# Two copies of a scratch image, zero rows around it, and products on all 128 rows

## The chip, the cores and the metric

The kernel runs on one core of a Trainium2 chip. The time is the device time of one launch in microseconds (us). The profile is one further execution, recorded by the hardware profiler. Engines are written as in the profile: PE (matrix products), DVE (vector), ACT (scalar), POOL (GpSimd), SP (which here only starts DMAs).

## The reference

Input `x` is 4 x 16 x 256 x 256 in float32. Two layers follow each other, each with a residual:

```python
x = x + _L0_conv_ref(_gn(x), conv_w, conv_b)          # _gn: group norm over 8 groups of 2 channels
x = x + _L1_conv_ref(_gn(x), base_w, spl_w, scaler, bias)

# layer 0: a 3x3 convolution 16 -> 400 gives 25 logits per channel and pixel
weights = softmax(out.reshape(N, C, 25, H, W), axis=2)
y = einsum('ncuij,ncuij->ncij', unfold5x5(x), weights)

# layer 1: a 3x3 convolution of silu, and of 8 cubic B-splines, of the normalised image
out = einsum('bjhwn,ijn->bihw', silu(patches), base_weight.sum(2))
out += einsum('bjhwns,ijns->bihw', b_splines(patches), (spline_weight * scaler).sum(2))
out += bias
```

## The kernel before

**Setup** (to about 108 us) loads the input, takes the statistics of the first norm, normalises the first image and prepares the weights: `wt` for the splines and `ws` for silu and the residual, both with 128 partitions.

**Layer 0** works in 64 strips: 4 images, 2 halves of 128 rows (one row per partition), 8 strips of 32 columns. Every four columns are one step, 512 in all. PE makes the logits, two products per column (L878 on `am`, L882 on `an`) into `lg`; ACT takes the exponential (L901) into `e`; POOL multiplies it by the shifted images `u` (L906); DVE sums numerator and denominator into `nd` (L738). Some steps later the strip is divided (ACT L752 and L754, DVE L758 to L760) and POOL subtracts it from the input's tile `xc` (L766), which then holds the first layer's result, x1. The products' operands come in chunks of eight columns, 256 of them, loaded two chunks ahead: `load_im` issues five DMAs (three of `am` at L686, two of `an` at L696) on SP's queue. Once per strip `load_u` issues five DMAs (L710), and `load_xc` one per four strips (L716), on the same queue. In between, pieces of the next image's normalisation are issued (`normalize`, lines up to L405, with loads at L288 to L319 on SP).

After every fourth strip `xc` is complete, with 128 rows x 16 channels x 128 columns. `store` (L820) writes it to the scratch `x1s`, 1 MB in rows of 512 B. Fifteen of these stores are issued on ACT's queue and the last on POOL's. ACT takes the statistics of the second norm from the same tile (L786). The DMAs that SP and ACT issue share eight semaphores in turn, in program order, so that a DMA waits until the one eight places before it has landed.

**Layer 1** works in 64 units of 16 rows of an image. All 128 partitions hold 16 channels x 8 spline knots of the unit's 18 rows. `load_x` (L988) loads them from `x1s` in two halves, the eight knots' copies by a dimension of step 0, into the first free of three tiles (`xta`, `xtb`, `xtc`); `load_tiles` (L1003) loads the rows once more into partitions 64 to 127 of `sl`, in four blocks of 16 partitions, block k with the rows of one of four row offsets in the order 0, 1, 3, 2. Rows outside the image are set to zero by POOL memsets (L999, L1023). Loads run two units ahead:

```python
xtt[n % 3][:, a - lo : z - lo, :],
rows(x1s[b], [[CP, C], [0, NS], [1, (z - a) * W]], u * RU - 1 + a),
```

ACT takes the distance to the knots (Abs, L1036), silu from the upper half of `sl` into its lower half (L1018), and parts of the splines (L164 to L167); DVE makes the rest (L159, L168 to L170) into `ring`. PE multiplies: 48 products on `ring` (L1082) and 12 on `sl` (L1092), these on 128 rows only for the middle column tap, where `ws` also adds the residual, else on 64. DVE adds the bias (L1065) and SP stores 2 x 128 KB (L1072).

`layer1` begins as layer 0 ends. The tile `xtc` lies where layer 0's `xc` tiles were, so its first load waits until the last store has landed. `scales` turns the second norm's statistics into per-partition factors `q` for every image, with one product on `sel` that spreads 16 channels over 128 partitions.

Of the kernel before, what the change touches and what calls it, by code (L numbers as in the profile page):

```python
# [4 lines left out]

# [30 lines left out]
def conv_preact_kernel(  # L36
# [12 lines left out]
    nc = tc.nc  # L49
    B, C, H, W = x.shape  # L50
    G = 8
    GC = C // G
    P = 128
# [6 lines left out]
    NS = 8  # L60
# [5 lines left out]
    CX = 128  # L66
# [6 lines left out]
    QG = 4  # L73
    RT = 2
    NT = P // (RT * C)
    RD = RT + 2
    RU = 16
    NU = H // RU
    SROWS = (0, 1, 3, 2)
    LAG1 = 2  # L80

    const = ctx.enter_context(tc.tile_pool(name="const", bufs=1))
# [5 lines left out]
    hsl = [[dram.tile([C, 2, CT], F32, name=f"hsl{b}_{h}") for h in range(NH)] for b in range(B)]  # L88

    CP = H * W + 1024  # L90
    x1s = [dram.tile([C, CP], F32, name=f"x1s{b}") for b in range(B)]
    ones = const.tile([P, P], F32, name="ones")
    nc.vector.memset(ones, 1.0 / P)
    mhalf = const.tile([P, G], F32, name="mhalf")
    nc.vector.memset(mhalf, -0.5)
    ub = const.tile([P, 1], F32, name="ub")
    ubrow = const.tile([1, C, NS], F32, name="ubrow")
    for s in range(NS):
        nc.vector.memset(ubrow[:, :, s : s + 1], 3.5 - s)
    ident = const.tile([P, P], F32, name="ident")  # L100
    make_identity(nc, ident)

    sel = const.tile([C, C, NS], F32, name="sel")
    nc.vector.tensor_copy(sel, ident[0:C, 0:C].unsqueeze(2).to_broadcast([C, C, NS]))
    onec = const.tile([P, 1], F32, name="onec")
    nc.vector.memset(onec, 1.0)
    flag = const.tile([1, 1], mybir.dt.int32, name="flag")
# [15 lines left out]
    ws = const.tile([P, 3, RT, C], F32, name="ws")  # L123
    nc.gpsimd.memset(ws, 0.0)
    for r in range(RT):
        p = P // 2 + SROWS.index(r + 1) * C
        nc.sync.dma_start(ws[p : p + C, 1, r], ident[p : p + C, p : p + C])

    edge = const.tile([P, 5], F32, name="edge")
    stat1 = ctx.enter_context(tc.tile_pool(name="stat1", bufs=1))  # L130
# [43 lines left out]
    def scales(b, psum):  # L174


        def small(n, name):
            return stat1.tile([P, n], F32, name=f"{name}_{b}", tag=f"{name}{b % 2}")

        sums, d, mz, p = small(2 * G, "sums"), small(G, "d"), small(G, "mz"), small(G, "p")  # L180
        q = stat1.tile([P, 6], F32, name=f"q_{b}", tag=f"q{b}")
        nc.vector.tensor_reduce(sums, st1[b].rearrange("p t g k -> p (t g) k"), AX.X, ALU.add)
        yield
        ps = psum()[:, 0 : 2 * G]
        nc.tensor.matmul(ps, lhsT=ones, rhs=sums, start=True, stop=True)
        yield
        part = 1.0 / (GC * CX * NK)
        nc.scalar.activation(d, ps[:, 0:G], AF.Square, scale=part)
        yield

        nc.vector.scalar_tensor_tensor(mz, ps[:, 0:G], part, nrm[b][:, 1], ALU.mult, ALU.subtract)
        nc.vector.scalar_tensor_tensor(d, ps[:, G : 2 * G], part, d, ALU.mult, ALU.subtract)  # L192
        yield
        nc.gpsimd.tensor_add(d, d, nrz[b][:, 1])  # L194
        nc.gpsimd.tensor_tensor(p, d, mhalf, ALU.pow)
        nc.gpsimd.tensor_mul(d, p, nrz[b][:, 0])
        nc.gpsimd.tensor_mul(p, p, gsel_sb)
        nc.gpsimd.tensor_mul(p, p, mz)
        yield
        nc.vector.reduce_sum(q[:, 0:1], d, AX.X)  # L200
        nc.vector.reduce_sum(q[:, 1:2], p, AX.X)
        nc.vector.tensor_scalar(q[:, 1:2], q[:, 1:2], -1.0, None, ALU.mult)
        for k in range(2):
            nc.vector.tensor_scalar(q[:, 2 + k : 3 + k], q[:, k : k + 1], 2.5, None, ALU.mult)
        yield
        ps = psum()[:, 0:2]
        nc.tensor.matmul(
            ps, lhsT=sel.rearrange("p c s -> p (c s)"), rhs=q[0:C, 2:4], start=True, stop=True
        )
        yield  # L210
        nc.vector.tensor_copy(q[:, 4:5], ps[:, 0:1])
        nc.vector.tensor_add(q[:, 5:6], ps[:, 1:2], ub)
        sc[b] = tuple(q[:, k : k + 1] for k in (0, 1, 4, 5))
        yield

    sc = {}
# [31 lines left out]
    def zeros(b, queue):  # L248

        for e in (0, HP - PAD):  # L250
            for r in range(PAD):
                yield partial(
                    queue.dma_start,
                    hs[b][:, e + r].rearrange("s c w -> c s w"),
                    zero[0:C, 0 : NST * SP].rearrange("c (s w) -> c s w", s=NST),
                )
        for h in range(NH):
            for w in (0, (W + 1) * RP):
                yield partial(queue.dma_start, hst[b][h][:, w : w + RP], zero[0:C, 0:RP])
                yield partial(  # L260
                    queue.dma_start,
                    hsl[b][h][:, :, w : w + RP].rearrange("c t r -> (c t) r"), zero[:, 0:RP],
                )
# [178 lines left out]
    with tc.tile_pool(name="prep0", bufs=2) as prep, tc.tile_pool(  # L442
# [42 lines left out]
        for d in range(3):  # L485
# [10 lines left out]

        ups = pstat.tile([P, 1], F32, name="ups", tag="hps")
        nc.tensor.matmul(
            ups, lhsT=ubrow.rearrange("p c s -> p (c s)"), rhs=onec[0:1], start=True, stop=True
        )  # L500
        nc.vector.tensor_copy(ub, ups)
        nc.scalar.activation(edge[:, 0:1], ub, AF.Abs)
# [31 lines left out]
        def prepare1():  # L534

            nc.gpsimd.tensor_mul(sw, sw, ss)
            wc = pre.tile([P, 3, nm], F32, name="wc")
            for d in range(3):
                nc.vector.tensor_reduce(
                    wc[:, d], sw[:, d].rearrange("p k j -> p j k"), AX.X, ALU.add  # L540
                )
            nc.vector.tensor_scalar(wc, wc, -1.0 / 6.0, None, ALU.mult)
            wb1 = pre.tile([nm, nm], F32, name="wb1")
            nc.vector.tensor_reduce(wb1, bw.rearrange("p k j -> p j k"), AX.X, ALU.add)
            for r in range(RT):
                nc.vector.tensor_copy(
                    wt[:, r : r + 3, :, r, :], wc.rearrange("p d (e o) -> p d e o", e=3)
                )
                for d in range(3):
                    p = SROWS.index(r + d) * C  # L550
                    nc.sync.dma_start(
                        ws[p : p + C, :, r, :],
                        wb1[d * C : (d + 1) * C].rearrange("p (e o) -> p e o", e=3),
                    )

# [102 lines left out]
    def layer0(shift):  # L658
# [4 lines left out]
        with tc.tile_pool(name=f"prep{arm}", bufs=2) as prep, tc.tile_pool(  # L663
# [150 lines left out]
            def store(n, xc):  # L814
                b, hf, s = strips[n]
                c0 = s * SW + SW - CX
                v = x1s[b][:, 0 : H * W].rearrange("c (p w) -> p c w", w=W)

                queue = nc.gpsimd if n == len(strips) - 1 else nc.scalar
                queue.dma_start(v[hf * P : (hf + 1) * P, :, c0 : c0 + CX], xc)  # L820


            nc.scalar.add_instruction(
# [107 lines left out]
    def layer1(arm, last, marks, seeds):  # L931
# [5 lines left out]
        with ExitStack() as pools:  # L937
# [46 lines left out]
            def load_x(n, half):  # L984
                b, u = units[n]
                lo, hs = halves(u)
                a, z = hs[half]
                nc.sync.dma_start(  # L988
                    xtt[n % 3][:, a - lo : z - lo, :],
                    rows(x1s[b], [[CP, C], [0, NS], [1, (z - a) * W]], u * RU - 1 + a),  # L990
                )

            def load_tiles(n):
                b, u = units[n]
                t = sl[n % 3][P // 2 :, :, 1 : W + 1]
                for p, q in outside(u):
                    nc.gpsimd.memset(t[p : p + C, q], 0.0)  # L999
                for k, d in enumerate(SROWS):  # L1000
                    q0 = 1 if (u, d) == (0, 0) else 0
                    q1 = RU // RT - (1 if (u, d) == (NU - 1, RD - 1) else 0)
                    nc.sync.dma_start(  # L1003
                        t[k * C : (k + 1) * C, q0:q1, :],
                        rows(x1s[b], [[CP, C], [RT * W, q1 - q0], [1, W]], u * RU - 1 + d + q0 * RT),
                    )

            def outside(u):

                return [  # L1010
                    (SROWS.index(d) * C, q)
                    for at, d, q in ((0, 0, 0), (NU - 1, RD - 1, RU // RT - 1)) if u == at
                ]

            def silu(n):
                b, u = units[n]
                t = sl[n % 3][0 : P // 2, :, 1 : W + 1]
                nc.scalar.activation(  # L1018
                    t, sl[n % 3][P // 2 :, :, 1 : W + 1], AF.Silu,
                    scale=sc[b][0][P // 2 :], bias=sc[b][1][P // 2 :],  # L1020
                )
                for p, q in outside(u):
                    nc.gpsimd.memset(t[p : p + C, q], 0.0)  # L1023

            def features(n, between):
                b, u = units[n]
# [49 lines left out]
            def outputs(n):  # L1076
# [11 lines left out]

                for e in range(3):
                    for t in range(NT):  # L1090
                        v = slice(0, P if e == 1 else P // 2)
                        nc.tensor.matmul(  # L1092
                            yp[t * M : (t + 1) * M],
                            lhsT=ws[v, e].rearrange("p r o -> p (r o)"),
                            rhs=sl[n % 3][v, t : t + NT + 1 : NT, e : e + W],
                            start=False, stop=e == 2,
                        )
                waiting.append((b, u, yp))
# [108 lines left out]
```

## Time and profile before

| | |
|---|---|
| median of 3 runs | 3049.09 us (3042.98 to 3049.54) |
| profiled execution, span | 3050.8 us |
| layer 0, about | 108 to 2040 us |
| layer 1, about | 2040 us to the end |
| busy PE, DVE, ACT, POOL | 2804.2, 2954.8, 2252.1, 1948.5 us |
| hardware DMA queue of SP and ACT | 320132 packets, 607.39 MB |

The page of the profile gives busy times, 40 slices of the span, the DMA queues, the chain of work that ended last and the costliest groups of instructions. Other views answer narrower questions: the waits of an engine (who ended them, total, how often, longest), the timeline, the chain in a window, and busy times by windows. L12 is line 12 of the kernel's file before.

```
PEclk7799999999999999999999999979999999999999
DMA  8988988878978778878857667659999999999993
```

These are two rows of the 40 slices: the granted TensorE clock and the mean busy share of the 16 DMA engines, in tenths.

### The profile page before, as it was taken

To read this page: it belongs to the slowest core of one execution; us is meant where nothing else is said; L and a number is where in the kernel's file an instruction comes from. 1 tells how busy PE (TensorE), PEld (TensorE's weight loads), DVE (VectorE), ACT (ScalarE), POOL (GpSimd) and SP (SyncE) were. 2 spreads that over 40 slices of the span, in tenths; PEclk is the share of its full clock that TensorE was granted. 3 is DMA by queue.
4 is the path that set the end of the run, shared out by engine and by line. 5 is a ranking of instruction groups with operands and counts; after the bars stand their busy time and mean duration, and the time that the engine had idled before them with its cause. 6 is when DMAs were issued, how large, how long until landed. Compare 5 with 4: busy or idle time off the path is not lost.

```text
span 3050.8 us, 39867 instructions
## 1 busy us (share of the span) xinstructions
PE 2804.2 (92%) x14280; PEld 1447.6 (47%) x14280; DVE 2954.8 (97%) x1587; ACT 2252.1 (74%) x2619; POOL 1948.5 (64%) x744
## 2 busy tenths in 40 slices
PE   4699999999989999999999999958999999999998
PEld 3465656656656666666666556632222222222222
DVE  7599999999999999999999999999999999999997
ACT  6566776576765666766645646559999999999996
POOL 4399999999999999999999999980100100000000
PEclk7799999999999999999999999979999999999999
DMA  8988988878978778878857667659999999999993
GB/s 274 254 232 223 261 238 238 230 196 247 244 207 229 201 207 226 241 209 228 234 152 194 179 165 191 162 128 208 201 192 195 195 195 190 199 195 199 192 199 86
DMA packets 353042, 628.40 MB, mean 206 GB/s; under 512 B 41394, under 2 KB 218788, under 8 KB 336964
## 3 DMA queue, kind: packets, MB, share of 16 engines
q1 hardware_dynamic: 320132, 607.39, 81.0%
q10 hardware_dynamic: 30960, 15.73, 1.7%
q8 instruction: 117, 1.92, 0.3%
q0 software_dynamic: 1744, 2.64, 0.3%
q14 instruction: 89, 0.73, 0.1%
HBM read 516.05 MB, written 104.24 MB: 203 GB/s over the span
## 4 chain that ended last, share of the span: by engine, by line
DVE 68%; issue 12%; PE 9%; DMA 5%; ACT 3%; POOL 2%; SPq 1%; DVEq 0%; POOLq 0%; ACTq 0%
DVE nd L738 43%; PE lg L878 6%; DVE ta L169 4%; DVE ta L168 4%; DVE tb L169 4%; DVE tb L168 4%; DVE tb L159 2%; PE lg L882 2%; DVE yo L1065 1%; POOL e L906 1%; DVE r L759 1%; DMA an<-hsl 1%; DVE nd L758 1%; DVE nd L760 1%; DVE lo L396 1%
## 5 line engine op out<-in xcount | busy, mean ns | idle before, releaser
L906 POOL TENSOR_TENSOR e<-e,u 128x1600 f32<-128x1600 f32 x512 | 1788.5, 3543 | 56.4 <-ACT e L901 49.0
L878 PE MATMUL lg<-wm,am 128*128 128x400 f32 x4096 | 1735.7, 505 | 80.3 <-ACT e L901 49.1
L738 DVE TENSOR_REDUCE nd<-e 128x128 f32<-128x3200 f32 x512 | 1749.2, 3478 | 24.3 <-POOL e L906 24.3
L882 PE MATMUL lg<-wn,an 97*128 97x400 f32 x2048 | 1344.3, 656 | 12.8 <-DMA an<-hsl 12.7
L901 ACT ACTIVATE e<-lg 128x800 f32<-128x800 f32 x1024 | 820.0, 837 | 682.8 <-DVE nd L738 440.7
L878 PEld LDWEIGHTS lg<-wm,am 128*128 128x128 f32 x4096 | 759.9, 192 | 400.1 <-ACT e L901 104.5
L1082 PE MATMUL yp<-ring,wt 128*32 128x512 f32 x6144 | 745.3, 597 | 86.6 <-DVE ring L170 62.6
L882 PEld LDWEIGHTS lg<-wn,an 97*128 97x128 f32 x2048 | 388.1, 190 | 330.7 <-issue 21.7
L1082 PEld LDWEIGHTS yp<-ring,wt 128*32 128x32 f32 x6144 | 202.2, 109 | 621.6 <-issue 433.1
L999 POOL MEMSET sl<- 16x256 f32 x6 | 1.8, 306 | 402.9 <-PE yp L1092 396.8
L169 DVE TENSOR_TENSOR ta<-ta,ta 128x2048 f32<-128x2048 f32 (+1 forms) x64 | 147.4, 2303 | 3.0 <-ACT ta L167 2.9
L170 DVE SCALAR_TENSOR_TENSOR ring<-ta,ta 128x2048 f32<-128x2048 f32 (+1 forms) x64 | 147.8, 2310 | 2.5
L786 ACT ACTIVATE z<-xc,nrm 128x256 f32<-128x256 f32 x240 | 144.2, 601 | 6.4 <-POOL xc L766 2.4
L170 DVE SCALAR_TENSOR_TENSOR ring<-tb,tb 128x2048 f32<-128x2048 f32 x64 | 145.6, 2275 | 2.5
L169 DVE TENSOR_TENSOR tb<-tb,tb 128x2048 f32<-128x2048 f32 x64 | 145.2, 2269 | 0.0
L1092 PE MATMUL yp<-sl,ws 64*32 64x512 f32 (+1 forms) x1032 | 131.2, 602 | 0.0
L999 POOL MEMSET slc<- 16x256 f32 x2 | 0.6, 309 | 203.1 <-PE yp L1092 203.0
L167 ACT ACTIVATE ta<-ta 128x2048 f32<-128x2048 f32 (+1 forms) x64 | 123.4, 1928 | 2.0
L194 POOL TENSOR_TENSOR d<-d,nrz 128x8 f32<-128x8 f32 x4 | 2.7, 680 | 189.9 <-DVE d L192 189.9
L167 ACT ACTIVATE tb<-tb 128x2048 f32<-128x2048 f32 x64 | 120.6, 1884 | 0.0
L1018 ACT ACTIVATE sl<-sl,q 64x2048 f32<-64x2048 f32 x43 | 90.0, 2094 | 1.2
L766 POOL TENSOR_TENSOR xc<-xc,nd 128x512 f32<-128x512 f32 x64 | 82.8, 1293 | 8.3 <-DVE nd L760 8.3
(200 smaller groups left out, 2108.8 us busy)
## 6 DMA issues: line engine op xcount, KB each, us to landing
am<-hst SPq DMA_DIRECT2D x512, 194.6 KB
u<-hs SPq DMA_DIRECT2D x320, 288.0 KB
an<-hsl SPq DMA_DIRECT2D x512, 129.8 KB
xta<-x1s SPq DMA_DIRECT2D x40, 1024.0 KB
xtb<-x1s SPq DMA_DIRECT2D x40, 1024.0 KB
xtc<-x1s SPq DMA_DIRECT2D x40, 1024.0 KB
am<-hst SPq DMA_DIRECT2D x256, 129.8 KB
sl<-x1s SPq DMA_DIRECT2D x166, 128.0 KB
```

Of the source, the lines that this page charges most:

```text
L167: nc.scalar.activation(s1, r1, AF.Square, scale=2.0)
L168: nc.vector.scalar_tensor_tensor(s2, t, 2.0, s2, ALU.subtract, ALU.mult)
L169: nc.vector.tensor_mul(s1, s1, r1)
L170: nc.vector.scalar_tensor_tensor(f, s2, 0.0, s1, ALU.min, ALU.subtract if given else ALU.add)
L738: nc.vector.tensor_reduce(nd[:, :, :, j : j + JG].rearrange("p t c j -> p t j c"), e.rearrange("p t j m c d -> p t j c m d"), AX.XY, ALU.add,)
L786: nc.scalar.activation(z, v, f, scale=nrm[b][:, 0, g : g + 1], bias=nrm[b][:, 1, g : g + 1], accum_out=st1[b][:, t, g, columns_of(n) : col ...
L878: nc.tensor.matmul(lg[:, i, :NL], lhsT=am[:, o : o + P], rhs=wm.rearrange("p m c d -> p (m c d)"), start=True, stop=False,)
L882: nc.tensor.matmul(lg[:, i, :NL], lhsT=an[:, o : o + P], rhs=wn.rearrange("p m c d -> p (m c d)"), start=False, stop=True,)
L901: nc.scalar.activation(ev, lg[:, :, :NL], AF.Exp)
L906: nc.gpsimd.tensor_tensor(e[:, 1].rearrange("p j m c d -> p j (m c) d"), e[:, 0].rearrange("p j m c d -> p j (m c) d"), uv, ALU.mult,)
L1082: nc.tensor.matmul(yp[t * M : (t + 1) * M], lhsT=wt[:, d, e].rearrange("p r o -> p (r o)"), rhs=ring[:, r0 + t * RT + d : r0 + t * RT + d ...
L1092: nc.tensor.matmul(yp[t * M : (t + 1) * M], lhsT=ws[v, e].rearrange("p r o -> p (r o)"), rhs=sl[n % 3][v, t : t + NT + 1 : NT, e : e + W], ...
```

## The change

- `x1s` has 32 rows of DRAM in place of 16, two copies of the 16 channels. `store` writes both, with two DMAs of 1 MB. The image begins one row (W) later, and `zeros` writes a zero row before it and one behind it for the first copy, one DMA per image.
- `load_x` reads from 32 rows, each spread over 4 partitions, in place of 16 spread over 8. The partitions' order changes from (channel, knot) to (copy, channel, knot of 4). `sel`, `ubrow` and the spline weights follow; the weights are permuted in setup by a product with `order`.
- `sl` holds its rows at partition 64 + 4c + d (channel c, row offset d). Its loads always take eight rows per offset, with the zero rows from DRAM; the POOL memsets go. In an image's first and last unit silu is done in two activations, the one for the outer rows with a scale and bias that are zero on the outside row's partitions (`inside`). `scales` makes four more columns of `q`, with two more DVE operations per image, and its product has four columns instead of two.
- The products on `sl` take all 128 rows for each of the three column taps; `ws` has zeros where nothing is to be added.

The core of the diff:

```diff
-    x1s = [dram.tile([C, CP], F32, name=f"x1s{b}") for b in range(B)]
+    x1s = [dram.tile([2 * C, CP], F32, name=f"x1s{b}") for b in range(B)]
...
-        ps = psum()[:, 0:2]
+        ps = psum()[:, 0:4]
...
-        nc.vector.tensor_copy(q[:, 4:5], ps[:, 0:1])
-        nc.vector.tensor_add(q[:, 5:6], ps[:, 1:2], ub)
-        sc[b] = tuple(q[:, k : k + 1] for k in (0, 1, 4, 5))
+        nc.vector.tensor_copy(q[:, 4:7], ps[:, 0:3])
+        nc.vector.tensor_add(q[:, 7:8], ps[:, 3:4], ub)
+        for k in range(2):
+            nc.vector.tensor_scalar(
+                q[:, 8 + 2 * k : 10 + 2 * k], ps[:, 0:2], inside[:, k : k + 1], None, ALU.mult
+            )
+        sc[b] = tuple(q[:, k : k + 1] for k in range(4, 12))
...
+        yield partial(
+            queue.dma_start,
+            bass.AP(
+                tensor=x1s[b].tensor, offset=x1s[b].offset,
+                ap=[[CP, C], [(H + 1) * W, 2], [1, W]],
+            ),
+            zero[0 : 2 * C, 0:W],
+        )
...
+            order = pre.tile([P, 2, C, SH], F32, name="order")
+            nc.vector.tensor_copy(order, ident.rearrange("p (c h s) -> p h c s", h=2, s=SH))
+            wcp = ptr0.tile([P, QG, P], F32, name="wcp", tag="tp").rearrange("p g w -> p (g w)")
+            wcp = wcp[:, 0 : 3 * nm]
+            nc.tensor.matmul(
+                wcp, lhsT=order.rearrange("p h c s -> p (h c s)"),
+                rhs=wc.rearrange("p d j -> p (d j)"), start=True, stop=True,
+            )
...
-                v = x1s[b][:, 0 : H * W].rearrange("c (p w) -> p c w", w=W)
+                v = x1s[b][:, W : W + H * W].rearrange("c (p w) -> p c w", w=W)
 
                 queue = nc.gpsimd if n == len(strips) - 1 else nc.scalar
-                queue.dma_start(v[hf * P : (hf + 1) * P, :, c0 : c0 + CX], xc)
+                for h in range(2):
+                    queue.dma_start(
+                        v[hf * P : (hf + 1) * P, h * C : (h + 1) * C, c0 : c0 + CX], xc
+                    )
...
-                    rows(x1s[b], [[CP, C], [0, NS], [1, (z - a) * W]], u * RU - 1 + a),
+                    rows(x1s[b], [[CP, 2 * C], [0, SH], [1, (z - a) * W]], u * RU + a),
...
-                t = sl[n % 3][P // 2 :, :, 1 : W + 1]
-                for p, q in outside(u):
-                    nc.gpsimd.memset(t[p : p + C, q], 0.0)
...
+                for d in range(RD):
                     nc.sync.dma_start(
+                        sl[n % 3][P // 2 + d : P : RD, :, 1 : W + 1],
+                        rows(x1s[b], [[CP, C], [RT * W, RU // RT], [1, W]], u * RU + d),
                     )
...
+                q0, q1 = 1 if u == 0 else 0, RU // RT - (1 if u == NU - 1 else 0)
+                for a, z, k in ((0, q0, 4), (q0, q1, 0), (q1, RU // RT, 6)):
+                    if a < z:
+                        nc.scalar.activation(
+                            sl[n % 3][0 : P // 2, a:z, 1 : W + 1],
+                            sl[n % 3][P // 2 :, a:z, 1 : W + 1], AF.Silu,
+                            scale=sc[b][k][P // 2 :], bias=sc[b][k + 1][P // 2 :],
+                        )
...
-                        v = slice(0, P if e == 1 else P // 2)
                         nc.tensor.matmul(
                             yp[t * M : (t + 1) * M],
-                            lhsT=ws[v, e].rearrange("p r o -> p (r o)"),
-                            rhs=sl[n % 3][v, t : t + NT + 1 : NT, e : e + W],
+                            lhsT=ws[:, e].rearrange("p r o -> p (r o)"),
+                            rhs=sl[n % 3][:, t : t + NT + 1 : NT, e : e + W],
```

More of the change, by code (lines that the diff above doesn't have):

```diff
@@ L2 @@
 from functools import partial
-from itertools import chain
 from itertools import chain
@@ L78, in conv_preact_kernel @@
     NU = H // RU
-    SROWS = (0, 1, 3, 2)
     LAG1 = 2
@@ L96, in conv_preact_kernel @@
     ub = const.tile([P, 1], F32, name="ub")
-    ubrow = const.tile([1, C, NS], F32, name="ubrow")
+    SH = NS // 2
+    ubrow = const.tile([1, 2, C, SH], F32, name="ubrow")
     for s in range(NS):
-        nc.vector.memset(ubrow[:, :, s : s + 1], 3.5 - s)
+        nc.vector.memset(ubrow[:, s // SH, :, s % SH : s % SH + 1], 3.5 - s)
     ident = const.tile([P, P], F32, name="ident")
     make_identity(nc, ident)
-    sel = const.tile([C, C, NS], F32, name="sel")
-    nc.vector.tensor_copy(sel, ident[0:C, 0:C].unsqueeze(2).to_broadcast([C, C, NS]))
+    sel = const.tile([C, 2, C, SH], F32, name="sel")
+    for h in range(2):
+        nc.vector.tensor_copy(sel[:, h], ident[0:C, 0:C].unsqueeze(2).to_broadcast([C, C, SH]))
+    inside = const.tile([P, 2], F32, name="inside")
+    for k, d in enumerate((0, RD - 1)):
+        nc.vector.reduce_sum(inside[:, k : k + 1], ident[:, d:P:RD], AX.X)
+    nc.vector.tensor_scalar(inside, inside, -1.0, 1.0, ALU.mult, ALU.add)
     onec = const.tile([P, 1], F32, name="onec")
@@ L125, in conv_preact_kernel @@
     for r in range(RT):
-        p = P // 2 + SROWS.index(r + 1) * C
-        nc.sync.dma_start(ws[p : p + C, 1, r], ident[p : p + C, p : p + C])
+        nc.sync.dma_start(ws[P // 2 + r + 1 : P : RD, 1, r], ident[0:C, 0:C])
     edge = const.tile([P, 5], F32, name="edge")
@@ L180, in scales @@
         sums, d, mz, p = small(2 * G, "sums"), small(G, "d"), small(G, "mz"), small(G, "p")
-        q = stat1.tile([P, 6], F32, name=f"q_{b}", tag=f"q{b}")
+        q = stat1.tile([P, 12], F32, name=f"q_{b}", tag=f"q{b}")
         nc.vector.tensor_reduce(sums, st1[b].rearrange("p t g k -> p (t g) k"), AX.X, ALU.add)
@@ L205, in scales @@
         yield
-        ps = psum()[:, 0:2]
+        ps = psum()[:, 0:4]
         nc.tensor.matmul(
-            ps, lhsT=sel.rearrange("p c s -> p (c s)"), rhs=q[0:C, 2:4], start=True, stop=True
+            ps, lhsT=sel.rearrange("p h c s -> p (h c s)"), rhs=q[0:C, 0:4], start=True, stop=True
         )
         yield
-        nc.vector.tensor_copy(q[:, 4:5], ps[:, 0:1])
-        nc.vector.tensor_add(q[:, 5:6], ps[:, 1:2], ub)
-        sc[b] = tuple(q[:, k : k + 1] for k in (0, 1, 4, 5))
+        nc.vector.tensor_copy(q[:, 4:7], ps[:, 0:3])
[5 more added lines that the diff above has]
+        sc[b] = tuple(q[:, k : k + 1] for k in range(4, 12))
         yield
@@ L498, in conv_preact_kernel @@
         nc.tensor.matmul(
-            ups, lhsT=ubrow.rearrange("p c s -> p (c s)"), rhs=onec[0:1], start=True, stop=True
+            ups, lhsT=ubrow.rearrange("p h c s -> p (h c s)"), rhs=onec[0:1],
+            start=True, stop=True,
         )
@@ L546, in prepare1 @@
                 nc.vector.tensor_copy(
-                    wt[:, r : r + 3, :, r, :], wc.rearrange("p d (e o) -> p d e o", e=3)
+                    wt[:, r : r + 3, :, r, :], wcp.rearrange("p (d e o) -> p d e o", d=3, e=3)
                 )
                 for d in range(3):
-                    p = SROWS.index(r + d) * C
                     nc.sync.dma_start(
-                        ws[p : p + C, :, r, :],
+                        ws[r + d : P // 2 : RD, :, r, :],
                         wb1[d * C : (d + 1) * C].rearrange("p (e o) -> p e o", e=3),
@@ L816, in store @@
                 c0 = s * SW + SW - CX
-                v = x1s[b][:, 0 : H * W].rearrange("c (p w) -> p c w", w=W)
+                v = x1s[b][:, W : W + H * W].rearrange("c (p w) -> p c w", w=W)
                 queue = nc.gpsimd if n == len(strips) - 1 else nc.scalar
-                queue.dma_start(v[hf * P : (hf + 1) * P, :, c0 : c0 + CX], xc)
+                for h in range(2):
+                    queue.dma_start(
+                        v[hf * P : (hf + 1) * P, h * C : (h + 1) * C, c0 : c0 + CX], xc
+                    )
             nc.scalar.add_instruction(
@@ L996, in load_tiles @@
                 b, u = units[n]
-                t = sl[n % 3][P // 2 :, :, 1 : W + 1]
-                for p, q in outside(u):
-                    nc.gpsimd.memset(t[p : p + C, q], 0.0)
-                for k, d in enumerate(SROWS):
-                    q0 = 1 if (u, d) == (0, 0) else 0
-                    q1 = RU // RT - (1 if (u, d) == (NU - 1, RD - 1) else 0)
+                for d in range(RD):
                     nc.sync.dma_start(
-                        t[k * C : (k + 1) * C, q0:q1, :],
-                        rows(x1s[b], [[CP, C], [RT * W, q1 - q0], [1, W]], u * RU - 1 + d + q0 * RT),
-                    )
[L1008 to L1013, printed above, removed]
+                        sl[n % 3][P // 2 + d : P : RD, :, 1 : W + 1],
+                        rows(x1s[b], [[CP, C], [RT * W, RU // RT], [1, W]], u * RU + d),
+                    )
             def silu(n):
                 b, u = units[n]
[L1017 to L1023, printed above, removed]
+                q0, q1 = 1 if u == 0 else 0, RU // RT - (1 if u == NU - 1 else 0)
[6 more added lines that the diff above has]
+                        )
             def features(n, between):
```

## The prediction

> **What bounds the kernel now.** I read the page first: busy times, the chain's shares, the costliest groups.
>
> ```profile
> PE 2804.2 (92%) x14280; PEld 1447.6 (47%) x14280; DVE 2954.8 (97%) x1587; ACT 2252.1 (74%) x2619; POOL 1948.5 (64%) x744
> ...
> DVE 68%; issue 12%; PE 9%; DMA 5%; ACT 3%; POOL 2%; SPq 1%; DVEq 0%; POOLq 0%; ACTq 0%
> ...
> L906 POOL TENSOR_TENSOR e<-e,u 128x1600 f32<-128x1600 f32 x512 | 1788.5, 3543 | 56.4 <-ACT e L901 49.0
> ...
> L738 DVE TENSOR_REDUCE nd<-e 128x128 f32<-128x3200 f32 x512 | 1749.2, 3478 | 24.3 <-POOL e L906 24.3
> ```
>
> DVE is busy 97% of the span and its reduce waits only 24.3 us for POOL in all. The shares average two stages, so the windows come next: one inside layer 0, three around one store of x1, one inside layer 1. Columns: length, busy PE, PEld, DVE, ACT, POOL, granted TensorE clock, DMA share, GB/s.
>
> ```profile
> 500.00:1000.00 500.00, 477.81 (x1680) 309.21 (x1679) 496.85 (x204) 325.61 (x565) 485.61 (x150) 0.99 0.83 222
> 664.00:669.00 5.00, 0.08 (x1) 0.00 (x0) 5.00 (x2) 3.48 (x10) 5.00 (x2) 0.89 1.07 179
> 669.00:676.00 7.00, 6.93 (x15) 4.23 (x16) 7.00 (x3) 2.30 (x5) 4.52 (x2) 0.59 0.96 169
> 676.00:690.00 14.00, 14.00 (x54) 9.36 (x52) 12.81 (x6) 10.87 (x20) 13.59 (x5) 1.00 0.75 225
> ...
> 2250.00:2500.00 250.00, 235.56 (x1957) 59.55 (x1960) 248.29 (x142) 248.12 (x117) 11.74 (x11) 1.00 0.96 194
> ```
>
> In layer 1 DVE (248.29 of 250) and ACT (248.12) run back to back, a unit every 15.25 us, while the DMA share is 0.96: the loads run just inside what the engines allow, so quicker loads have at most 1.7 us per 250 to give. In layer 0 DVE and POOL are both nearly full, so what one loses is hardly caught up. After a store, PE stands still for 5 us and then runs at a clock of 0.59. The waits of SP's queue between 130 and 2000 us say why:
>
> ```profile
> SPq L710 <- DMA x1s<-xc: 106.5, 11, 10.8
> SPq L696 <- DMA x1s<-xc: 36.3, 3, 12.7
> ...
> SPq L686 <- DMA x1s<-xc: 13.6, 1, 13.6
> ```
>
> All loads of layer 0 stand in SP's one queue, in order. Semaphores go round eight at a time over the DMAs of SP and ACT together, so the eighth DMA behind a store waits until the store has landed: 15 times, 156 us. One of them in SP's timeline, and in the chain of 640 to 700 us:
>
> ```profile
> 645.49 12.95 SPq L710 DMA_DIRECT2D u<-hs  x5
> ```
> ```profile
> 660.25 8.68 DMA am<-hst
> 669.07 1.67 PE lg L878 x2
> ...
> 678.03 0.67 PE lg L878 x2
> ```
>
> The store is issued on ACT at 652.66 and lands 4.5 us later; only then do the next chunk's loads go out. They land 8.7 us after issue, and a PE pair takes 1.67 us cold for 0.67 warm.
>
> **Layer 0: a second store behind each store.** It is another 1 MB in 512-B packets. Those took 27 ns, 128 on each of 16 engines: 3.46 us, plus 0.37 us of issue on ACT (hidden: ACT is 65% busy there). SP is now held twice: one DMA earlier for the first copy, then for the second. The next chunk's loads come later by δ. [...] At the most it is 3.46 plus a further turn of the queue: 4. A δ below zero is excluded, since bytes and waits are only added. What δ costs I read store by store, as the margin by which the logits after it could be later before DVE waits (ends of PE's groups and POOL's products against the start of DVE's reduce). Stores 0, 1, 2, 3, 5, 7, 9 have 1.05, 1.63, 0.58, 0.20, 0.90, 0.87, 1.14 us; the eight others 4.5 to 6.1. Summing δ minus margin where positive: 3.7 us for δ = 1.4, 12.5 for 2.7 (the middle), 21.6 for 4.
>
> There is a second term. PE's longest gap after each store is 4.1, 3.7, 1.9, 5.0, 1.5, 2.6, 1.5, 3.6, 1.7, 1.8, 1.5, 1.3, 0.7, 1.1, 0.9 us, and a low clock follows only the four of 3.6 and more; it costs about 3.3 us of PE time (the 7 us at 0.59 above, with some catching up). A δ of 2.7 lifts ten more gaps to some 3.6 or more; with 3.3 us added at these, the sum is 25.4 (δ = 1.4: 7.0; δ = 4: 44.7). Whether a gap just past 3.6 is already punished isn't shown, so I take the middle of 12.5 and 25.4: **+19**.
>
> [...]
>
> **The seam.** In layer 1's first units ACT waits three times for loads (waits of 2030 to 2130 us):
>
> ```profile
> ACT xtb L1036 <- DMA xtb<-x1s: 6.3, 1, 6.3
> ...
> ACT L1018 <- DMA sl<-x1s: 5.3, 1, 5.3
> ACT xtc L1036 <- DMA xtc<-x1s: 5.1, 1, 5.1
> DVE tb L159 <- ACT xtc L1036: 3.2, 1, 3.2
> ```
>
> The chain goes through the third: the last store (POOL's queue, 2057.42, landing in 5.38) releases the load of xtc, whose two 1-MB halves land 5.05 us apart. The last store is now two: +3.46 us. Whether 32 DRAM rows speed the load's 8192-B packets (600 ns median now) the trace can't show. At best they run at the rate of the 2304-B packets of u, whose DRAM side has 128 rows (93 ns, so 331 ns for 8192 B), and the two halves save 2 × 5.05 × (1 − 331/600) = 4.5, net −1.0; unchanged, +3.4. I take half-way: **+1**.
>
> **Layer 1, steady.** Faster loads are worth nothing where DVE and ACT never wait; slower ones would show at once: above 4% (1/0.96) each further 1% costs some 9 us of 920, and that is the upper bound of the unknown rate. Nothing in the trace has more rows and longer packets, so I take no loss. Eight silus become two activations. 64x2048 takes 2.09 us, 128x4096 3.81, so the fixed part is at most 0.4 us each, 3 in all; it lies in ACT's lead over DVE, which grows from 3.8 to 8.3 us. Products on 128 rows: L1092 took 604 ns with 128 rows, 601 with 64, and PE isn't the bound. POOL's memsets that go were off the path (POOL busy 11.74 of 250). Two more tiny DVE operations per batch, 0.07 us each, two batches inside the layer: **+0.3**. If ACT's cover were gone, 3 us.
>
> **Setup and tail.** A few DVE operations, one PE product and a DMA of zero rows beside ACT's statistics and the input's loads, which end setup; the three later zero DMAs are 0.6 us of SP each amid 526 us in which SP waits for PE. POOL now also issues setup's first one. **0 to +1**, taken 0.3. The tail is PE's, unchanged.
>
> **Sum.** 19 + 1 + 0.3 + 0.3 = 20.6 us. The profiled execution has a span of 3050.8, 1.7 over the median of the runs, 3049.09; the differences are put on the median: 3069.7.
>
> **Rivals.** *The second store is hidden* (chance 0.17): δ at or below 1.4 and no new cold gap, so 3.7 + 1 + 0.6: 3054, within what a measurement can tell, about 0.2% or 6 us. For it: eight of fifteen stores have 4.5 us or more of margin. Against it: a DMA share of 1.07 right after a store.
>
> *Faster* (0.08): the loads decide. If 8-KB packets fall to 331 ns and δ is under 1 (sum 1.5), the seam's third wait shrinks: DVE begins that unit at 2079.8 and could at 2074.9, a gain of up to 4.9; with all of DVE's idle time of the steady window, 1.71 of 250, over 920 us, 6.3 more: 3049 − 11 + 1.5, some 3040. It decides only if the packets fall below 400 ns and SP's waits on stores hardly grow; against it stands 248.29 of 250.
>
> *Every gap cold* (0.06): δ = 4 with the clock, 44.7, and the seam's +3.4: 3098.
>
> *The load doesn't change* (inside the forecast): two copies leave the packets at 600 ns; the seam takes its +3.4, layer 0 stays: 3072.
>
> **Numbers.** The forecast (second store late by 1.4 to 4, part of the gaps cold, 3055 to 3095) has 0.69. The range 3047 to 3095 takes in the hidden store and leaves out the faster case and the coldest one. Faster by over 0.2%: 0.07; within 0.2%: 0.18, the hidden store and the rest of the faster case; slower: 0.75.
>
> **What would show it.** Right: SP's waits on x1s<-xc grow from 156 to over 230 us in about 30 times; PE's waits on am and an exceed 16.3 and 12.2; DVE's wait at L738 for POOL grows from 24.3 to 40 or more; more windows under clock 0.7 after stores; layer 1 starts some 20 us later and keeps 15.25 us a unit. Wrong: L738's wait unchanged (hidden); a longer period with a DMA share near 1.00 in layer 1 (the loads got slower); or a shorter period.

## The result and the profile after

The change takes 3071.15 us (median of 4 runs, 3069.19 to 3072.66) against 3049.05 before: 1.0071 of it, 95% interval 1.0057 to 1.0086. Measured again, beside the experiments on the place in DRAM below, it was 1.0053 (1.0038 to 1.0069). The forecast, 3069.7 us, was met in size and sign. Its reason was met only in part. The loss takes two things together: the second store, which the forecast priced, and a shift of 160 bytes in SBUF, which it did not see. Leave out either and most of the loss is gone.

The profiled execution has a span of 3067.4 us, 16.6 more than that of before. That is less than the 22 us between the medians, because the profiled execution of before lies above that kernel's median and the one of after is the fastest of its runs. The page after, the lines that answer to those of before (the reduce is now L762, the product L933):

```profile
PE 2776.0 (91%) x14282; PEld 1490.6 (49%) x14282; DVE 2959.6 (96%) x1600; ACT 2263.3 (74%) x2627; POOL 1956.8 (64%) x730
...
DVE 50%; ACT 29%; issue 7%; PE 5%; DMA 5%; POOL 3%; SPq 1%; ACTq 0%; POOLq 0%; DVEq 0%
...
L933 POOL TENSOR_TENSOR e<-e,u 128x1600 f32<-128x1600 f32 x512 | 1789.8, 3558 | 72.8 <-ACT e L928 53.2
...
L762 DVE TENSOR_REDUCE nd<-e 128x128 f32<-128x3200 f32 x512 | 1751.1, 3479 | 37.2 <-POOL e L933 37.0
```

DVE does the same work; its reduce waits 12.7 us longer for POOL (24.3 to 37.0), and POOL's product stands idle 16.4 us longer (56.4 to 72.8), by the profile before ACT's exponential and before loads of `an` and `am`. These totals hold the first steps too; from step 8 on the reduce waits 19.1 us in place of 4.1 (worked out from the traces). The waits of SP's queue and of PE on loads, 130 to 2030 us (who waited, for whom; total, times, longest):

```profile
SPq L734 <- DMA x1s<-xc: 126.4, 17, 12.1
SPq L710 <- DMA x1s<-xc: 41.0, 8, 15.5
SPq L720 <- DMA x1s<-xc: 28.0, 2, 14.0
```
```profile
PE lg L905 <- DMA am<-hst: 39.1, 15, 6.3
...
PE lg L909 <- DMA an<-hsl: 12.0, 11, 4.7
```

SP is held by the stores for 201 us in 30 times (two small groups included) instead of 156 in 15, and PE waits 39.1 us for `am` in place of 16.3. To see where the time goes, I set the start of the same DVE instruction in both traces against each other. This is worked out from the traces, in us after minus before:

```
reduce of step 8   48     64     80     96     224    320    352    511 | unit 2  unit 63 | end
       -0.7       +0.6   +2.5   +4.2   +6.1   +8.7  +12.7  +15.5  +17.0 | +16.9   +17.6  | +16.6
```

The loss comes right behind single stores: 1.8 to 3.6 us each within 10 steps (38 us) of stores 0, 1, 5, 8 and 9, about 1 us behind 2, 7 and 12, next to nothing in between. Layer 0 costs 17.7 us from step 8 on, the seam 0, layer 1 0.75. The loads of layer 1 meanwhile became much lighter. Same columns as in the windows of before:

```profile
2250.00:2500.00 250.00, 225.07 (x1960) 70.13 (x1956) 248.54 (x144) 248.12 (x119) 10.15 (x7) 0.96 0.58 197
```

The DMA share falls from 0.96 to 0.58 at the same bytes, since the median of the 8192-B packets goes from 600 to 309 ns (the estimate's best case was 331) and that of the 1024-B packets (loads of `sl`, stores of the output) from 65 to 46 (2100 to 2900 us); the unit still takes 15.25 us.

### The profile page after: what moved, and what is told of

The parts are those of the page before. It is cut to its first block, busy times and chain, and to the rows that moved or that the text cites. A ratio compares the mean times of both kernels' runs of the same rounds, so it can differ in the third digit from the quotient of the medians.

```text
span 3067.4 us, 39879 instructions
## 1 busy us (share of the span) xinstructions
PE 2776.0 (91%) x14282; PEld 1490.6 (49%) x14282; DVE 2959.6 (96%) x1600; ACT 2263.3 (74%) x2627; POOL 1956.8 (64%) x730
## 4 chain that ended last, share of the span: by engine, by line
DVE 50%; ACT 29%; issue 7%; PE 5%; DMA 5%; POOL 3%; SPq 1%; ACTq 0%; POOLq 0%; DVEq 0%
DVE nd L762 44%; ACT ta L168 4%; ACT ta L170 3%; ACT tb L168 3%; ACT tb L171 3%; PE lg L905 3%; POOL e L933 2%; ACT sl L1033 2%; ACT xtb L1050 2%; ACT xta L1050 2%; ACT xtc L1050 2%; ACT ta L171 2%; DVE r L783 1%; ACT slc L1033 1%; DMA x1s<-xc 1%
## 5 line engine op out<-in xcount | busy, mean ns | idle before, releaser
L933 POOL TENSOR_TENSOR e<-e,u 128x1600 f32<-128x1600 f32 x512 | 1789.8, 3558 | 72.8 <-ACT e L928 53.2
L905 PE MATMUL lg<-wm,am 128*128 128x400 f32 x4096 | 1747.9, 508 | 84.5 <-DMA am<-hst 39.1
L762 DVE TENSOR_REDUCE nd<-e 128x128 f32<-128x3200 f32 x512 | 1751.1, 3479 | 37.2 <-POOL e L933 37.0
L909 PE MATMUL lg<-wn,an 97*128 97x400 f32 x2048 | 1351.4, 660 | 12.2 <-DMA an<-hsl 12.0
L928 ACT ACTIVATE e<-lg 128x800 f32<-128x800 f32 x1024 | 832.4, 838 | 683.0 <-PE lg L909 360.0
L905 PEld LDWEIGHTS lg<-wm,am 128*128 128x128 f32 x4096 | 767.7, 194 | 402.7 <-ACT e L928 73.2
L1096 PE MATMUL yp<-ring,wt 128*32 128x512 f32 x6144 | 781.0, 625 | 129.2 <-DVE ring L174 106.2
L1096 PEld LDWEIGHTS yp<-ring,wt 128*32 128x32 f32 x6144 | 222.5, 113 | 637.0 <-issue 441.8
L1105 PE MATMUL yp<-sl,ws 128*32 128x512 f32 x1032 | 152.9, 591 | 0.0
L1033 ACT ACTIVATE sl<-sl,q 64x2048 f32<-64x2048 f32 (+2 forms) x49 | 91.7, 1883 | 1.1
L1050 ACT ACTIVATE xtc<-xtc,q 128x4096 f32<-128x4096 f32 (+2 forms) x21 | 80.0, 3808 | 10.6 <-DMA xtc<-x1s 10.0
```

Of the source, the lines that this page charges most:

```text
L762: nc.vector.tensor_reduce(nd[:, :, :, j : j + JG].rearrange("p t c j -> p t j c"), e.rearrange("p t j m c d -> p t j c m d"), AX.XY, ALU.add,)
L905: nc.tensor.matmul(lg[:, i, :NL], lhsT=am[:, o : o + P], rhs=wm.rearrange("p m c d -> p (m c d)"), start=True, stop=False,)
L909: nc.tensor.matmul(lg[:, i, :NL], lhsT=an[:, o : o + P], rhs=wn.rearrange("p m c d -> p (m c d)"), start=False, stop=True,)
L928: nc.scalar.activation(ev, lg[:, :, :NL], AF.Exp)
L933: nc.gpsimd.tensor_tensor(e[:, 1].rearrange("p j m c d -> p j (m c) d"), e[:, 0].rearrange("p j m c d -> p j (m c) d"), uv, ALU.mult,)
L1033: nc.scalar.activation(sl[n % 3][0 : P // 2, a:z, 1 : W + 1], sl[n % 3][P // 2 :, a:z, 1 : W + 1], AF.Silu, scale=sc[b][k][P // 2 :], bias ...
```

## The experiments

Theory at the start: the second store behind each store in layer 0. Rivals: the silu side (zero rows, split silu, products on 128 rows), and the wait alone rather than the bytes. Each ratio compares with runs of the kernel before on the same chip, taken beside it. "Layer 0" below is the drift of DVE's reduces against the trace of before from step 8 to the last, which leaves out the first steps, whose start differs by some us from execution to execution; "landing" is from a store's issue to its last semaphore update, both from the trace's DMA records, like the mean of the stores' 512-B packets. The drift is of one execution each: where no loss was to be expected it came to -1.5 and +0.8 us, so 1 or 2 us of it mean little.

**The silu side alone.** Everything but the second copy, the 32-row loads and the new order of partitions.

```diff
-                for h in range(2):
-                    queue.dma_start(
-                        v[hf * P : (hf + 1) * P, h * C : (h + 1) * C, c0 : c0 + CX], xc
-                    )
+                queue.dma_start(v[hf * P : (hf + 1) * P, :, c0 : c0 + CX], xc)
...
-                    rows(x1s[b], [[CP, 2 * C], [0, SH], [1, (z - a) * W]], u * RU + a),
+                    rows(x1s[b], [[CP, C], [0, NS], [1, (z - a) * W]], u * RU + a),
```

> The change without its second copy: one store per tile, loads from 16 rows, partitions in the old order; the zero rows, the interleaved sl, the split silus and the products on 128 rows stay. Theory (the second store in layer 0 is the cost): layer 0 ends within 2 us of before, layer 1 shows the 0.5 us per image boundary of the split silus, in all +0 to +3 us: about 3050. Rival (the silu side or the zero rows cost the time): 3065 or more. The 8-KB packets of the loads stay near 600 ns.

Measured 1.0013 (1.0002 to 1.0024): layer 0 +4.9 us, layer 1 about +1.6. The size is near the theory's, but the +4.9 stood where nothing had been expected: one store, as before, yet it landed after 5.05 us, not 4.5, and its packets took 28.7 ns, not 27.0. So without its second store the change loses some 4 us (6 by the medians), not 22.

**A second store in the kernel before**, into a scratch `x2s` that nobody reads, in full and with 8 KB only.

```diff
                 queue.dma_start(v[hf * P : (hf + 1) * P, :, c0 : c0 + CX], xc)
+                queue.dma_start(v2[hf * P : (hf + 1) * P, :, c0 : c0 + CX], xc)
```
```diff
+                queue.dma_start(v2[hf * P : hf * P + 16, 0:1, c0 : c0 + CX], xc[0:16, 0:1])
```

> The kernel before with a second 1-MB store of each tile, into a scratch that nobody reads. Theory (second store): +17 to +22 us, all of it in steps after the stores in layer 0: about 3068. Rival (silu side): within 3 us of before. SP's waits on x1 stores rise from 156 us to some 195 or more in about 27 times.

> As the run with a second 1-MB store into an unread scratch, but only 16 partitions of one channel, 8 KB, are written the second time. The place in the queue and the further turn of the semaphores stay, the bytes go. Theory as predicted (the 3.46 us of packets make the loads late): at most +5 us, about 3052. Rival (the further wait itself, with SP held one DMA earlier, makes them late): +12 us or more.

The full one came to 1.0029 (1.0010 to 1.0047), some 9 us, and in its profile layer 0 lost only 1.6. The tiny one came to 1.0010 (0.9998 to 1.0023), layer 0 +1.3. So the theory's 17 to 22 us were not there: the full one's two stores landed after 4.5 and 7.3 to 7.7 us, against 5.2 and 8.9 to 9.3 (once 10.6) in the change. SP was held 188 us in 30 times, near what was expected, and yet little of it arrived at DVE. The full one's profile, of a run of 3054.6 among 3051 to 3082, shows some 5 us more that the theory did not contain, half at the seam and half in the first units of layer 1; the rest of the 9 us it doesn't show.

**The second store on POOL's queue.**

```diff
-                    queue.dma_start(
+                    (nc.gpsimd if h else queue).dma_start(
```

> The change with the second copy's store issued on POOL's queue in place of ACT's, so that SP waits for the first copy alone; the bytes stay, and POOL pays some 1.3 us of issue 15 times. If the time is made by SP's second wait: back to +3 to +8 us. If the 1 MB on the same 16 engines makes it, wherever it is issued: +14 us or more, and SP's waits on the first store become longer than before's 10.4 us each.

Measured 1.0090 (1.0073 to 1.0108), worse than the change: layer 0 +27.2 us. SP waits for one store only (170 us in 15 times), so its second wait is no necessary part of the loss. The store now starts 4 to 10 us later and lands 6.7 to 12.2 us after its issue, and POOL, nearly as full as DVE (485.6 and 496.9 of 500 us in the window of before inside layer 0), pays the issue (1.26 us for the one store that it issues in the trace of before). Which of the two costs more was not separated.

**Where a slow store comes from: the place in DRAM.** The stores were slow in all kernels with the image one row into the scratch and fast in the others, so I moved it: 4 KB in place of 1 KB in the change (XO is 1024 elements), and 1 KB alone in the kernel before. The change itself ran beside them.

```diff
-                v = x1s[b][:, W : W + H * W].rearrange("c (p w) -> p c w", w=W)
+                v = x1s[b][0 : 2 * C, XO : XO + H * W].rearrange("c (p w) -> p c w", w=W)
```
```diff
-                v = x1s[b][:, 0 : H * W].rearrange("c (p w) -> p c w", w=W)
+                v = x1s[b][:, W : W + H * W].rearrange("c (p w) -> p c w", w=W)
```

> The change with the image 4 KB into each scratch row in place of one image row (1 KB); the zero rows move with it, both copies stay. In the run with a second store into an unread scratch the two stores landed 4.5 and 7.4 us after issue and layer 0 moved little; in the change they land 5.2 and 9.1 us after it. Theory now (the 1-KB shift makes the stores slow, and that pushes the loads past DVE's margin): stores at about 4.5 and 7.5 us, layer 0 within 6 us of before, in all 3050 to 3056. Rival (two stores into one tensor are slow, or the second store's bytes are the cost anyway): stores at 5 and 9 us, 3065 or more.

> The kernel before with the image one row (1 KB) into each scratch row and nothing else. Theory (the shift makes each store slow): stores land 5.05 us after issue in place of 4.5, as in the run of the silu side alone, and layer 0 loses 2 to 5 us. Rival (the zero rows' DMAs or the silu side do it): stores at 4.5 us and no loss in layer 0.

> The change itself, for its time beside the others of this call. Both theories: 1.005 to 1.009 of before.

This theory fell on both sides: 1.0060 (1.0044 to 1.0075) with stores at 5.2 and 9.1 us in the first, 0.9999 (0.9986 to 1.0013) with stores at 4.5 us in the second. The change came to 1.0053.

**One copy, loads in two DMAs of 64 partitions.**

```diff
+                for h in range(2):
+                    nc.sync.dma_start(
+                        xtt[n % 3][h * P // 2 : (h + 1) * P // 2, a - lo : z - lo, :],
+                        rows(x1s[b], [[CP, C], [0, SH], [1, (z - a) * W]], u * RU + a + XO // W - 1),
+                    )
```

> The change with the image 4 KB into each row and one copy only: one store per tile, and each half of a load as two DMAs of 64 partitions that read the same 16 rows, each row spread over 4 partitions. If the loads were slow because two DMA engines read one DRAM row side by side: 8-KB packets near 310 ns as in the change, a DMA share of some 0.6 in layer 1, stores at 4.5 us, and a time of 3044 to 3051. If 32 distinct rows are needed: packets of 500 ns or more and a share above 0.85.

1.0005 (0.9994 to 1.0016). The 8-KB packets stayed at 592 ns in the median: sixteen rows, though spread over four partitions in each DMA, are not what made the change's loads fast. The share fell to 0.81 all the same; it was 0.84 already with the silu side alone, where the 1024-B packets took 46 ns in place of 65. Here too the one store landed late, after 5.05 us, and layer 0 lost 7.1.

**The place in SBUF.** All the kernels with slow stores have something else in common: the larger `q` (4 x 32 bytes per partition) and the new tile `inside` push every tile behind them 160 bytes on. `xc`, which a store reads in 512-B pieces, lies at 198144 in the program before, a multiple of 512, and at 198304 in the change. So I put an unused tile among the constants: 352 bytes in the change, which brings `xc` to 198656, again a multiple of 512; 160 bytes in the kernel before, which brings it to the change's place; and 352 in the kernel with one copy.

```diff
+    const.tile([P, 88], F32, name="gap")
     inside = const.tile([P, 2], F32, name="inside")
```
```diff
+    const.tile([P, 40], F32, name="gap")
     onec = const.tile([P, 1], F32, name="onec")
```

> The change with 352 bytes of unused constants per partition in SBUF, so that xc lies at a multiple of 512 B again (198144 before, 198304 in the change, 198656 here). The shift by one row in DRAM turned out not to matter (stores stayed at 4.5 us), nor did the 4-KB place (5.2 and 9.1 us). Theory now (xc's place in SBUF makes each 512-B packet of a store slow): stores land 4.5 and some 7.5 us after issue, packets 27 ns, layer 0 loses 1 to 6 us instead of 17: 1.001 to 1.004 of before. Rival (the two copies, or the zero rows, cost it): stores at 5.2 and 9.1 us, 1.005 or more.

> The kernel before with 160 bytes of unused constants per partition, so that xc lies at 198304 as in the change. Theory (place in SBUF): stores land 5.05 us after issue, packets 28.7 ns, layer 0 loses 2 to 5 us as with the silu side alone; 1.0005 to 1.002. Rival: stores at 4.5 us and no loss.

> One copy, each half of a load in two DMAs of 64 partitions (share 0.81 in layer 1 in its first run), and xc back at a multiple of 512 B. Theory (place in SBUF): stores at 4.5 us, layer 0 as before, layer 1 free of waits for loads: 0.998 to 1.001, at best 5 us under before. Rival: stores at 5.05 us and 1.0005 to 1.0015 as in its first run.

With 352 unused bytes the change takes 0.9995 of before (0.9984 to 1.0006), where 1.001 to 1.004 had been expected: the loss is gone, with both copies, both stores, zero rows and all the rest still in it. The stores land after 4.5 and 7.1 to 7.6 us, with packets of 27.0 ns. Its waits of SP and PE, in the views shown of the change above:

```profile
SPq L735 <- DMA x1s<-xc: 117.8, 17, 11.4
...
SPq L711 <- DMA x1s<-xc: 37.1, 8, 14.9
SPq L721 <- DMA x1s<-xc: 26.6, 2, 13.3
```
```profile
PE lg L906 <- DMA am<-hst: 16.8, 6, 4.6
PE lg L910 <- DMA an<-hsl: 9.5, 12, 3.4
```

SP is held as often as in the change (30 times) and for nearly as long (186 us); but PE waits for `am` 16.8 us, as before, not 39.1. The chains from 405 to 440 us, around the second pair of stores, first of the change, then of the change with the gap (start, length, what):

```profile
414.52 5.19 DMA x1s<-xc
...
421.85 5.13 DMA am<-hst
```
```profile
413.89 4.49 DMA x1s<-xc
...
419.72 4.62 DMA am<-hst
```

Counted from the first store's issue, the next chunk's `am` is under way 7.3 us later in the one and 5.8 in the other, and is in after 12.5 and 10.5 us. Behind this store layer 0 lost 3.6 us in the change and 1.3 with the gap, and TensorE's granted clock, the third column from the end, was 0.91 in the one and 0.96 in the other. The windows 410 to 450 us of the change and of the change with the gap:

```profile
410.00:450.00 40.00, 32.06 (x108) 20.17 (x107) 37.27 (x17) 30.76 (x69) 31.47 (x10) 0.91 0.90 236
```
```profile
410.00:450.00 40.00, 34.03 (x117) 21.43 (x116) 39.39 (x17) 32.51 (x70) 33.80 (x11) 0.96 0.94 261
```

The kernel before with the change's place took 1.0021 (1.0007 to 1.0034), with its stores at 5.05 us and packets of 28.8 ns; layer 0 lost 4.2 us. The kernel with one copy took 0.9994 (0.9985 to 1.0004), its stores at 4.5 us, layer 0 +0.8.

Set side by side, these runs show what one store and two cost at each place. All have the change's silu side; times against the kernel before:

| | `xc` at a multiple of 256 B | `xc` 160 B past one |
|---|---|---|
| one store | 0.9994 (one copy, gap) | 1.0005 (one copy), 1.0013 (silu side) |
| two stores | 0.9995 (change, gap) | 1.0060 (change, 4 KB), 1.0053 (change) |

The two kernels in the middle column ran beside each other, and so did the one-copy kernel and both with two stores on the right. The second store costs 0.3 us by the medians in the middle (3049.5 to 3049.8) and 14 to 16 us on the right (3053.0 to 3067.2 and 3069.1). The pairs differ in layer 1's loads too, but in none of these traces did ACT or DVE wait for those past the first units. So the loss belongs neither to the second store alone nor to the place alone.

What the place does to the stores it does to other transfers as well: the 512-B packets that load `xc` took 32 ns in the median at 198304 and 27 at the other places. That load is no part of the steps behind the stores, since it is issued 27 to 40 us behind each store, by when nearly the whole step has been lost.

**A multiple of 256 or of 512.** The change with 96 unused bytes: `xc` at 198400.

```diff
+    const.tile([P, 24], F32, name="gap")
```

> The change with 96 bytes of unused constants per partition, so that xc lies at 198400, a multiple of 256 B but not of 512 B. If what counts is where a packet starts within 256 B: stores at 4.5 and some 7.4 us, packets 27 ns, 0.998 to 1.002 of before, as with 352 bytes. If a 512-B packet has to start at a multiple of 512 B: stores at about 5.2 and 9.1 us and 1.005 or more.

Measured 0.9983 (0.9971 to 0.9996), stores at 4.5 and 7.1 to 7.8 us, packets of 27.0 ns. At 198400, a multiple of 256 B but not of 512, the packets were as short as at 198656. Whether a multiple of 64 or 128 would do was not run: 198304 is a multiple of 32 alone. The time is 4.4 us under the kernel before by the medians, the lowest ratio of the study, though its interval overlaps that of the gap of 352 bytes.

## Why the prediction was right, and where its reason was wrong

**The chain from a late store to DVE was right.** The loss is in layer 0, in steps behind the stores, by SP's queue, `am`, PE and its clock, POOL, DVE. PE's longest gap behind a store rose at 13 of 15 of them (in sum from 33 to 53 us), and the ones of 3.6 us and more from four to eight, where ten more had been counted.

**One reading of the clock was wrong.** A low clock followed not only the four gaps of 3.6 us and more: in the trace of before the granted clock was 0.50 for 3.4 us or longer behind seven stores, three of them with longest gaps of 1.8, 1.9 and 2.6 us. One of these windows, behind store 2, where PE had stood idle twice, for 1.89 and 1.43 us:

```profile
551.80:555.20 3.40, 3.40 (x8) 2.08 (x7) 3.40 (x2) 0.84 (x1) 2.27 (x1) 0.50 1.04 172
```

So the longest gap alone doesn't tell where the clock falls, and no threshold is shown here. Low clock within 40 us of the stores, in all: 31 us at seven of them before, 75 at twelve in the change, 41 at nine in the change with the gap. Elsewhere in layer 0 it came to 0 to 45 us a trace, in kernels with and without the loss.

**The term that was mis-sized is the delay δ: "It is another 1 MB in 512-B packets. Those took 27 ns".** The row was that of before, and the packets of the change took 30.9 ns on average. With packets of 27.0 ns the second store is real, its waits on SP are real, and little of it arrives at the end: layer 0 lost 1.6 to 3.4 us in three traces, and the change with the gap takes 0.9995. That figure is a net one, as its profile has 2 us less at the seam. The delay δ of the next chunk's `am` behind the first store, from issue to landing against before, in the mean of the 15 stores, is 1.0 us there and 2.9 in the change (worked out from the traces). My δ of 2.7, the middle between 1.4 and 4, hit what the change has, for a reason that I had not seen: I made it of the second store's 3.46 us alone, and in the run some 1.9 us of it come from the longer packets of both stores, the pair landing after 9.1 us in place of 7.3. δ at 27 ns lies just below the low end of 1.4. No run shows the term that this low end was made with, the time ahead of a load's first packet: in the trace of before, loads that found SP's queue empty had their first packet 0.9 to 1.4 us after their issue in layer 0 (91 of them, median 1.33, worked out from the trace), and in the change the first load behind each first store had it after 3.2 to 3.9 us, as the second store's packets were ending. So with the place unchanged the hidden-store rival, which had 0.17, would have been right about the time, and the size of the forecast was luck in this term.

**The table of margins held in sum, not store by store.** At δ of 1.0 it gives 1.5 us and the run with the gap lost 3.2 in layer 0; at 2.9 it gives 13.9 before anything is added for the clock, and the change lost 17.7. But store 3, with the smallest margin, lost 0.1 us, and store 8, with over 4.5, lost 3.2.

**The parts don't add up to the whole.** In layer 0 the place alone, with one store, cost 4.2 to 7.1 us, the second store alone 1.6 to 3.4, both together 16.8 to 18.9 (three traces). That only together they pass the margins and bring the low clock fits the counts above; it was not tested apart.

**ACT's share.** The issue of the second store was put at 0.37 us. It took 1.6 to 1.9 us in the change and 1.2 to 1.7 with the gap, where the kernel takes no longer than before.

**SP's waits** were to exceed 230 us and were 201. The count, 30, was right. As the run with the gap has nearly the same waits and no loss, this sign alone would have proved nothing. Two more signs fell short: DVE's wait for POOL, to reach 40 us, reached 37.0, and PE's wait for `an`, to exceed 12.2, was 12.0.

**The seam** was put at +1 and was 0: `xtc` waits 10.0 us in place of 5.1, the two loads before it 6.3 in place of 11.6.

```profile
ACT xtc L1050 <- DMA xtc<-x1s: 10.0, 1, 10.0
...
ACT L1033 <- DMA sl<-x1s: 3.7, 1, 3.7
ACT xtb L1050 <- DMA xtb<-x1s: 2.6, 1, 2.6
```

**Layer 1** was put at +0.3 and was +0.75, in steps at the image boundaries, where ACT takes 0.53 us more for two units. That lighter loads are worth nothing there was right for the executions compared; a limit of that reading showed in two experiments. The tiny second store and the kernel before with 160 bytes, both with loads of 16 rows, fell 8.7 and 7.3 us further behind between units 6 and 17. Window 2140 to 2320 us of the tiny store:

```profile
2140.00:2320.00 180.00, 164.39 (x1332) 43.25 (x1332) 171.50 (x100) 169.56 (x80) 11.11 (x11) 0.97 1.00 186
```

The DMA share is 1.00 and ACT is idle for 10 of 180 us, by its waits for `sl` (10.1 us in all). No kernel with loads of 32 rows showed that, but neither did those with 16 rows and the change's loads of `sl` (silu side alone, one copy: share 0.78 to 0.84). So lighter loads buy safety from a bound that the loads of before, at a share of 0.96, sit just under, not time in each execution; that it takes the 32 rows is not shown.

**Setup and the products on 128 rows** cost nothing that shows, as expected.

## What to carry to other kernels

When a change adds or enlarges a constant, look at where the tiles behind it have moved: a tile that DMAs read in pieces of 512 B did best here at a multiple of 256 B (27.0 ns a packet, against 28.7 to 30.9 at 160 B past one), and 96 unused bytes bought that back. Before a loss is put down to an added transfer, compare how long its packets take with those of the kernel before; if they differ, something else has changed with it. A forecast whose range was spanned by bounds can hit the number by another cause, and only a run that adds the suspected cost alone, and one that takes it away alone, tell the two apart. And where two changes meet, as here, it takes all four combinations.

## What was new about the hardware

A store's 512-B packets took 27.0 ns each, nearly without spread, where `xc` began at a multiple of 256 B (198144, 198400, 198656), and 28.7 to 28.8 ns at 198304, which is 160 B past one; with two stores in a row there, 30.8 to 30.9. The landing of one store went from 4.5 to 5.05 us, of a pair from 7.4 to 9.1. The 512-B packets that load `xc` went from 27 to 32 ns in the median at the same place. That is 7 and 14% more for the stores' packets and 18% for those of the load. One place off a multiple of 256 B was run, so neither the cause of the longer packets nor 256 B as the unit is shown. The gap moves `u` and `am` with `xc`, and their share in the loss was not separated; the median packet of `u` went from 93 to 95 ns, that of `am` and `an` from 267 to 275.

A load that spreads 32 rows of DRAM over 128 partitions moved its 8192-B packets in 309 ns, one that spreads 16 rows in 600, and in 586 to 592 where the 16 rows went to 64 partitions in each of two DMAs (medians). Moving the image in DRAM, by 1 KB in the kernel before and from 1 to 4 KB in the change, changed nothing that shows.
